# Graph attention on one core: sums of exponentials folded onto half of the partitions by an accumulating transfer, and values half a step later

## The chip, the cores and the metric

The kernel runs on one core of one Trainium2 chip. The core has a matrix engine (TensorE, PE in the profile; PEld is its loading of weights), three engines for elementwise work (VectorE or DVE, ScalarE or ACT, GpSimd or POOL), a queue engine for transfers (SyncE, SP) and sixteen DMA engines that move data. The engines run side by side, each through its own list of instructions in order, and wait for each other by semaphores. SBUF is the working memory, PSUM the memory that TensorE writes; both have 128 partitions. The metric is the time of one execution on the device in microseconds (us). The median of three runs of the kernel before is 3563.94 us (3558.51 to 3566.34).

## The reference, cut to what matters

Two layers over 8 graphs (batches) of N = 2048 nodes with 256 features, all float32. Layer 0 is an attention with 4 heads of 64 features. Its softmax is taken apart over 8 chunks of 256 keys, and the 8 results are added:

```
h = relu(layernorm(x))
q, k, v = h @ Wq.T, h @ Wk.T, h @ Wv.T                 # per head: [N, 64]
scores = clip(q @ kc.T / 8, -10, 10)                   # per chunk j of 256 keys: [N, 256]
scores = where(mask == 0, -10, scores)
attn = softmax(scores, axis=-1)                        # over the 256 keys of one chunk
ctx = sum over j of attn_j @ vc_j                      # [N, 64] per head
x = x + layernorm(ctx @ Wo.T + h) * gamma + beta
```

Layer 1 is a graph attention with one head: weights made of a source and a target term per node, masked by the adjacency, times `h @ W`; its result is added to x.

## The kernel before, in words

**Steps.** For each batch the attention is done in 32 steps: 4 blocks of 512 queries (`nb`) times 8 chunks of 256 keys (`j`). The logits of a step stand transposed: keys on the partitions, queries along the row. A chunk has two key tiles of 128 (`kt`). For one head (`o`, in the order `ORDER`) and one key tile, `logits` (L481) issues four matmuls, each of which reads 64 partitions of k and q (the 64 features of the head) and writes 32 partitions of PSUM. The two heads of a pair lie on partitions 0 to 63 and 64 to 127, so the matmuls of one head occupy one half of TensorE's rows. A float32 matmul is two records in the profile.

**After the logits.** `clip` (L525, VectorE) takes the 128x1024 logits of a head out of PSUM, clips them and applies the mask in one instruction. `exponentials` (L535, ScalarE) works in place. `add` (L541, GpSimd) adds the two key tiles of two heads at a time, 128x1024, into a tile `both` for `sums` (L513): matmuls of 64 partitions each with a matrix of ones give the sum of the exponentials of each head. `values` (L495) multiplies the exponentials by v, again 64 partitions (`half`) at a time and 32 partitions of PSUM per head; the 64 features of a head are two such pieces (`c`), accumulated in two PSUM banks over both halves and both key tiles. `invert` (L547, ScalarE) makes 1/sum by a logarithm and an exponential, `scale` (L553, VectorE) multiplies the values by it, and `gather` (L562) adds the product to the context of the block by a transfer from GpSimd's queue that adds in passing (512 KB). PSUM holds two tiles of logits (`ps_s`), two banks of values (`ps_n`) and two others (`ps_t`).

**The order.** It is written by hand: each engine runs its instructions in the order in which the program issues them. `begin(f)` and `end(f)` (L597, L629) are the two halves of a step: logits of step f-1, half of the values and the sums of step f-2, the other half of the values of step f-3. As two row halves of TensorE must not write one PSUM bank at once, the values of half 0 and half 1 go to different banks and are exchanged in the second turn; `fence` (L460) puts a wait in between. The work between the layers (`Between`, L673) for the block before, and in the first batch half of the search of the adjacency (L312) and the next batch's norms, are pieces with a half-step number `n` in `todo` (L839 and L1127); a piece runs at the end of `begin` or `end`, or ahead of it (`first`, `pe`, `pe1`). For one block these are, by half-step from its end: 5 and 6 `bias`, 8 and 10 `beta`, 18 and 20 `add` on GpSimd; `stats` (two instructions per tile of 128x256), `take` and `flip1` on VectorE; `scaled` and `norm1` on ScalarE; `output_tiled` on TensorE. A block has 16 half-steps, so the blocks 1 to 3 of a batch have pieces and block 0 none but those of the first batch.

**Between the attentions.** After step 31 come the rest of layer 0, then layer 1 (`Layer1.products`, L956) whose matmuls read a tile `g` of [128, 16 x 257]. During its last products `early` (L570) issues the first logits, clips and exponentials of the next batch.

Of the kernel before, what the change touches and what calls it, by code (L numbers as in the profile page):

```python
# [24 lines left out]
SHIFT = 30.0  # L25


@with_exitstack
def gnn_two_layers(
# [97 lines left out]
    class Turning:  # L127
# [3 lines left out]
        def __init__(self, dst, tag):  # L131
            self.dst = dst
            self.squares = work.tile([P, FC * QUADS, TB, Q], F32, tag=tag, name="squares", bufs=3 if tag == "hT" else 2)
# [50 lines left out]
    g = const.tile([P, NT, F + 1], F32, name="g")  # L184
    nc.gpsimd.memset(g[:, :, F:F + 1], 1.0)
# [14 lines left out]
    def load_x(b, nb, tag, bufs):  # L200
        pool = work if tag == "both" else xpool
        t = pool.tile([P, TB, F], F32, tag=tag, name=tag, bufs=bufs)
        nc.sync.dma_start(t, x[b, nb * NB:(nb + 1) * NB, :].rearrange("(p t) f -> p t f", p=P))
        return t

# [61 lines left out]
    def missing_of(rows, t, half):  # L267

        tag = "e" if in_setup[0] else "hn"
        z = work.tile([P, 2 if in_setup[0] else 1, HALF], BF16, tag=tag, name="z", bufs=5)  # L270
# [24 lines left out]
    def keep_bounds(pt, t, half):  # L295

        nb, rows, cols = t // TB, slice(half * 8, (half + 1) * 8), slice((t % TB) * P, (t % TB + 1) * P)
        if nb in bounds:
            dst = bounds[nb][:, rows, cols]
        else:  # L300
            tag = part_tags[(2 * t + half) % 4] if in_setup[0] else "r"
            dst = work.tile([P, 8, P], I8, tag=tag, name="bound_part", bufs=2 if tag == "r" else 1)
# [11 lines left out]
    def adjacency(parts):  # L314
# [15 lines left out]
        turns = [12, 12, 18, 18, 26, 26, 32, 32]  # L330
# [15 lines left out]
    def norm_power(mv, rn):  # L346

        nc.scalar.activation(rn[:, 0, :], mv[:, :, 1], AF.Ln, bias=eps)
        nc.scalar.activation(rn[:, 0, :], rn[:, 0, :], AF.Exp, scale=-0.5)
        nc.scalar.activation(rn[:, 1, :], rn[:, 0, :], AF.Copy, scale=-1.0)  # L350
# [28 lines left out]
    class Projection:  # L379
# [6 lines left out]
        def load(self, nb):  # L386
            self.x[nb] = load_x(self.b, nb, *(("both", 2) if in_setup[0] else ("xp", 1)))
# [81 lines left out]
    class Attention:  # L469
        STEPS = [(nb, j) for nb in range(NNB) for j in range(NCH)]  # L470
# [3 lines left out]
        def __init__(self, proj):  # L474
            self.q, self.k, self.v = proj.q, proj.k, proj.v
            self.before, self.rest = {}, ()
            self.s, self.e, self.both, self.num, self.total, self.rz, self.prod, self.ctxT = ({} for _ in range(8))


# [15 lines left out]
        def values(self, n, half, c, kt):  # L495

            nb, j = self.STEPS[n]
            rows = slice(half * DH, (half + 1) * DH)
            started = (n, c) in self.num
            if not started:  # L500
                self.num[n, c] = ps_n()
            made = []
            for h in range(HEADS):
                p, i = divmod(h, 2)
# [3 lines left out]
                    self.e[n, p][rows, i * KT + kt, :],  # L508
                    start=not started, stop=half == (1 if c else 0) and kt == KT - 1,
                ))  # L510
            return made

        def sums(self, n, half):  # L513
            rows = slice(half * DH, (half + 1) * DH)
            if half:
                self.total[n] = ps_t()
            return [
                nc.tensor.matmul(  # L518
                    self.total[n][h * Q:(h + 1) * Q, :], ones[rows, :], self.both[n, h // 2][rows, h % 2, :],
                    start=half == 1, stop=half == 0,  # L520
                )
                for h in range(HEADS)
            ]

        def clip(self, n, o):  # L525
            nb, j = self.STEPS[n]
            p, i = self.ORDER[o]
            if (n, p) not in self.e:
                self.e[n, p] = work.tile([P, 2 * KT, NB], F32, tag="e", name="e", bufs=5)
            nc.vector.scalar_tensor_tensor(  # L530
                self.e[n, p][:, i * KT:(i + 1) * KT, :], self.s.pop((n, o)), -CLIP * SC,
# [3 lines left out]
        def exponentials(self, n, o):  # L535

            p, i = self.ORDER[o]
            e = self.e[n, p][:, i * KT:(i + 1) * KT, :]
            nc.scalar.activation(e, e, AF.Exp, scale=1.0 / SC)  # L539

        def add(self, n, p):  # L541

            self.both[n, p] = work.tile([P, 2, NB], F32, tag="both", name="both")
            e = self.e[n, p].rearrange("p (i k) q -> p k i q", k=KT)
            nc.gpsimd.tensor_tensor(self.both[n, p], e[:, 0], e[:, 1], op=ALU.add)  # L545

        def invert(self, n):  # L547

            rz = self.rz[n] = work.tile([P, NB], F32, tag="rz", name="rz", bufs=1)
            nc.scalar.activation(rz, self.total.pop(n), AF.Ln)  # L550
            nc.scalar.activation(rz, rz, AF.Exp, scale=-1.0)  # L551

        def scale(self, n, c):  # L553
            nb, j = self.STEPS[n]
            if j == 0 and c == 0:
                self.ctxT[nb] = work.tile([P, 2, NB], F32, tag="ctx", name="ctxT")
            if j > 0 and c == 0:
                self.prod[n] = work.tile([P, 2, NB], F32, tag="prod", name="prod", bufs=1)
            dst = self.ctxT[nb] if j == 0 else self.prod[n]
            nc.vector.tensor_tensor(dst[:, c, :], self.num.pop((n, c)), self.rz[n], op=ALU.mult)  # L560

        def gather(self, n):  # L562
            nb, j = self.STEPS[n]
            if j > 0:
                nc.gpsimd.dma_start(self.ctxT[nb], self.prod.pop(n), accum_op=ALU.add)  # L565
# [4 lines left out]
        def early(self, part):  # L570
# [12 lines left out]
            elif part == 2:  # L583
                self.clip(0, 2)
                self.exponentials(0, 2)
                self.clip(0, 3)
                self.add(0, 0)
            if part == 3:
                for kt in range(KT):
                    self.logits(1, 0, kt)  # L590

        def begin(self, f, pieces=()):  # L597

            self.run(pieces, "first")
            if self.has(f - 3):  # L600
                made = {}
                for kt in range(KT):
                    for half, c in ((0, 0), (1, 1)):
                        made.setdefault(c, []).extend(self.values(f - 3, half, c, kt))
                for c in range(2):
                    fence(self.before.pop((f - 3, c)), made[c])
            if self.has(f - 1):
                self.clip(f - 1, 0)
            if self.has(f - 3):
                self.invert(f - 3)  # L610
            if self.has(f - 2):
                self.exponentials(f - 2, 3)
            if self.has(f - 1):
                self.exponentials(f - 1, 0)
            self.run(pieces, "pe")
            if self.has(f - 1):
                for kt in range(KT):
                    self.logits(f - 1, 1, kt)
                    self.logits(f - 1, 2, kt)
            if self.has(f - 3):  # L620
                self.scale(f - 3, 0)
                self.scale(f - 3, 1)
            if self.has(f - 2):
                self.add(f - 2, 1)
            if self.has(f - 3):
                self.gather(f - 3)
            self.rest = pieces

        def end(self, f, pieces=()):  # L629
            self.run(pieces, "first")  # L630
            if self.has(f - 1):
                self.clip(f - 1, 1)
            self.run(pieces, "pe1")
            if self.has(f - 1):
                self.clip(f - 1, 2)
            self.run(pieces, "after")
            self.run(self.rest, None)
            if self.has(f - 1):
                self.exponentials(f - 1, 1)
                self.exponentials(f - 1, 2)  # L640
            if self.has(f - 2):
                made = {}
                for kt in range(KT):
                    for half, c in ((0, 1), (1, 0)):
                        made.setdefault(c, []).extend(self.values(f - 2, half, c, kt))
                for c in range(2):
                    self.before[f - 2, c] = made[c]
            if self.has(f - 1):
                self.logits(f - 1, 3, 0)
            if self.has(f - 2):  # L650
                sums = self.sums(f - 2, 1)
            if self.has(f - 1):
                self.logits(f - 1, 3, 1)
            if self.has(f):
                self.logits(f, 0, 0)
            self.run(pieces, None)
            self.run(pieces, "pe")
            if self.has(f - 2):
                fence(sums, self.sums(f - 2, 0))
            if self.has(f):  # L660
                self.logits(f, 0, 1)
            if self.has(f - 1):
                self.clip(f - 1, 3)
                self.add(f - 1, 0)
# [8 lines left out]
    class Between:  # L673
# [66 lines left out]
        def power(self):  # L740
            norm_power(self.mv, self.rn)

        def shift(self):
            norm_shift(self.adder, self.mv, self.rn)

        def scaled(self, tiles):
            for t in tiles:
                o = self.o4[:, t, :]
                nc.scalar.activation(
                    o, o, AF.Identity, bias=self.rn[:, 1, t:t + 1], scale=self.rn[:, 0, t:t + 1]  # L750
                )

        def gamma(self, t2):
            o = self.o4[:, 2 * t2:2 * t2 + 2, :]
            self.adder.tensor_tensor(o, o, gamma_r[:, None, :].to_broadcast([P, 2, F]), op=ALU.mult)
# [35 lines left out]
        def flip1(self, t2, tag="hT"):  # L791
            if t2 == 0:
                self.aside = tag == "both"
# [605 lines left out]
```

## Time and profile before

| What | us |
|---|---|
| median of three runs | 3563.94 |
| the profiled execution | 3563.89 |
| its span, first to last instruction | 3562.1 |
| TensorE busy | 3527.6 |
| VectorE busy | 2639.0 |
| ScalarE busy | 1947.4 |
| GpSimd busy | 1808.9 |
| one step of the attention, without pieces on TensorE | 7.72 |
| a step with half of `output_tiled` | 9.45 |
| layer 1's products, per batch | 117.4 |

How to read it. A group line gives the line of the kernel, the engine, the operation, the names written and read, the shape and the count; then the busy time of the group, the mean ns of one, and the engine's idle time just before them with what ended it. A timeline line gives the start, the length, the engine, the line, the operation and how many of them follow each other; in brackets stands the idle time before it and who ended that. A line with two times and a colon is one stretch: its length, the busy time of PE, PEld, DVE, ACT and POOL, the granted TensorE clock (1.00 is full), the share of the DMA engines that was busy, and GB/s. Matmuls are pipelined; many of their records overlap.

### The profile page before, as it was taken

The page shows a single profiled execution, that of the slowest core. Times are in us where ns is not written, and L with a number is a line of the kernel's source. Part 1 is how long each engine was busy: PE and PEld are TensorE (multiplying, and loading weights), DVE is VectorE, ACT ScalarE, POOL GpSimd, SP SyncE. Part 2 cuts the span into 40 slices and gives each one's busy share as a digit, 9 for nine tenths or more (in the row PEclk, how much of TensorE's full clock was granted, in tenths as well). Part 3 has the DMA queues.
Part 4 walks back from the last instruction along what each step waited for, and adds up shares of the span by engine and source line. Part 5 has one row for each costly group of instructions (what it writes and reads, how often), then busy time and mean ns, then how long its engine had stood idle before and what let it go on. Part 6 is the DMA issues. An engine that isn't in the chain of part 4 may idle for free.

```text
span 3562.1 us, 104433 instructions
## 1 busy us (share of the span) xinstructions
PE 3527.6 (99%) x46080; PEld 2183.0 (61%) x46080; DVE 2639.0 (74%) x3979; ACT 1947.4 (55%) x2961; POOL 1808.9 (51%) x1182
## 2 busy tenths in 40 slices
PE   8999999999999999999999999999999999999999
PEld 5455785557755577555775557655586555855568
DVE  7888677867678676786767867678586785757866
ACT  6677426763267633676236762367624766147750
POOL 2688016870278702786037850378404784048731
PEclk9999999999999999999999999999999999999999
DMA  7545423444234441344423444234442434124321
GB/s 234 119 107 134 87 74 85 91 113 91 80 79 85 123 95 60 85 96 109 92 66 85 97 110 91 71 79 91 120 103 55 91 81 118 57 55 91 85 69 48
DMA packets 169111, 329.74 MB, mean 93 GB/s; under 512 B 35664, under 2 KB 97360, under 8 KB 160464
## 3 DMA queue, kind: packets, MB, share of 16 engines
q1 hardware_dynamic: 127696, 203.51, 19.2%
q0 software_dynamic: 32640, 118.50, 18.0%
q8 instruction: 360, 5.90, 0.7%
q10 hardware_dynamic: 8320, 1.05, 0.2%
q14 instruction: 95, 0.78, 0.1%
HBM read 154.14 MB, written 51.43 MB: 58 GB/s over the span
## 4 chain that ended last, share of the span: by engine, by line
PE 97%; DVE 1%; DMA 1%; ACT 1%; issue 0%; POOL 0%; ACTq 0%; DVEq 0%; POOLq 0%; SPq 0%
PE ps_s L490 25%; PE ps_n L506 24%; PE ps_s L963 12%; PE ps_t L518 7%; PE ps_n L963 6%; PE ps_t L963 6%; PE ps_t L714 2%; PE ps_t L434 2%; PE ps_n L434 2%; PE ps_s L434 2%; PE ps_t L814 2%; PE ps_n L814 2%; PE ps_t L448 1%; PE ps_n L448 1%; DVE z L277 0%
## 5 line engine op out<-in xcount | busy, mean ns | idle before, releaser
L530 DVE SCALAR_TENSOR_TENSOR e<-ps_s,bound 128x1024 f32<-128x1024 f32 x1024 | 1224.1, 1220 | 404.0 <-PE ps_s L490 400.6
L545 POOL TENSOR_TENSOR both<-e 128x1024 f32<-128x1024 f32 x512 | 1219.8, 2407 | 571.1 <-PE ps_t L518 355.6
L490 PE MATMUL ps_s<-q,k 64*32 64x512 f32 x16384 | 1431.8, 590 | 1.5 <-DVE e L530 1.4
L539 ACT ACTIVATE e<-e 128x1024 f32<-128x1024 f32 x1024 | 1050.6, 1050 | 481.1 <-DVE e L530 462.7
L506 PE MATMUL ps_n<-e,v 64*32 64x512 f32 x16384 | 1224.9, 591 | 2.4 <-DVE prod L560 2.4
L506 PEld LDWEIGHTS ps_n<-e,v 64*32 64x32 f32 x16384 | 460.9, 107 | 473.1 <-issue 384.1
L490 PEld LDWEIGHTS ps_s<-q,k 64*32 64x32 f32 x16384 | 459.5, 106 | 448.6 <-issue 331.2
L518 PE MATMUL ps_t<-both,ones 64*32 64x512 f32 x4096 | 537.9, 592 | 0.1
L963 PE MATMUL ps_s<-g,w 128*128 128x257 f32 x2048 | 447.8, 380 | 0.0
L963 PEld LDWEIGHTS ps_s<-g,w 128*128 128x128 f32 x2048 | 388.8, 190 | 56.3
L560 DVE TENSOR_TENSOR prod<-ps_n,rz 128x512 f32<-128x512 f32 x448 | 288.5, 686 | 162.8 <-PE ps_n L506 96.1
L986 POOL TENSOR_TENSOR x<-x,r 128x256 f32<-128x256 f32 x124 | 90.7, 745 | 466.2 <-ACT r L984 465.4
L946 DVE SCALAR_TENSOR_TENSOR w<-bound,w 128x1024 f32<-128x1024 int8 x256 | 314.7, 1229 | 8.7
L354 POOL TENSOR_TENSOR krn<-krn,mv 128x4 f32<-128x4 f32 x28 | 6.8, 242 | 575.4 <-DVE w L940 575.4
L963 PE MATMUL ps_n<-g,w 128*128 128x257 f32 x1024 | 292.4, 382 | 0.0
L963 PE MATMUL ps_t<-g,w 128*128 128x257 f32 x1024 | 289.7, 380 | 0.0
L550 ACT ACTIVATE rz<-ps_t 128x512 f32<-128x512 f32 x256 | 152.6, 596 | 229.4 <-PE ps_t L518 201.5
L940 DVE TENSOR_SCALAR w<-src,cd 128x512 f32<-128x512 f32 x512 | 263.1, 556 | 7.0 <-ACT src L921 6.6
L963 PEld LDWEIGHTS ps_n<-g,w 128*128 128x128 f32 x1024 | 192.8, 190 | 44.3 <-issue 17.6
L565 POOL DMA_DIRECT2D ctxT<-prod x224 | 191.0, 853 | 54.1 <-DVE prod L560 46.7
L963 PEld LDWEIGHTS ps_t<-g,w 128*128 128x128 f32 x1024 | 193.8, 189 | 28.2
L551 ACT ACTIVATE rz<-rz 128x512 f32<-128x512 f32 x256 | 161.4, 630 | 8.2
(133 smaller groups left out, 2910.4 us busy)
## 6 DMA issues: line engine op xcount, KB each, us to landing
ctxT<-prod POOLq DMA_DIRECT2D x224, 512.0 KB, 4.9
bound<-bound_d SPq DMA_DIRECT2D x62, 1024.0 KB, 6.2
turned_d<-squares SPq DMA_DIRECT2D x232, 128.0 KB, 2.4
hT<-turned_d SPq DMA_DIRECT2D x58, 512.0 KB, 4.3
rows<-in_adj_dram SPq DMA_DIRECT2D x32, 512.0 KB, 5.3
x<-in_x_dram SPq DMA_DIRECT2D x32, 512.0 KB, 4.9
out_dram<-x SPq DMA_DIRECT2D x31, 512.0 KB, 2.6
xp<-in_x_dram SPq DMA_DIRECT2D x28, 512.0 KB, 4.5
```

The source lines that it names most:

```text
L434: nc.tensor.matmul(in_key_order(pp) if i == 0 else pp, w[:, di, do * P:(do + 1) * P], h, start=di == 0, stop=di == FC - 1,)
L490: nc.tensor.matmul(self.s[n, o][c * Q:(c + 1) * Q, kt, :], self.k[p][rows, at:at + Q], self.q[p][rows, nb * NB:(nb + 1) * NB], start=True, ...
L506: made.append(nc.tensor.matmul(self.num[n, c][h * Q:(h + 1) * Q, :], self.v[rows, j * KT + kt, at:at + Q], self.e[n, p][rows, i * KT + kt, :],
L518: nc.tensor.matmul(self.total[n][h * Q:(h + 1) * Q, :], ones[rows, :], self.both[n, h // 2][rows, h % 2, :], start=half == 1, stop=half == 0,)
L530: nc.vector.scalar_tensor_tensor(self.e[n, p][:, i * KT:(i + 1) * KT, :], self.s.pop((n, o)), -CLIP * SC, bounds[nb][:, j * KT:(j + 1) * K ...
L539: nc.scalar.activation(e, e, AF.Exp, scale=1.0 / SC)
L545: nc.gpsimd.tensor_tensor(self.both[n, p], e[:, 0], e[:, 1], op=ALU.add)
L560: nc.vector.tensor_tensor(dst[:, c, :], self.num.pop((n, c)), self.rz[n], op=ALU.mult)
L565: nc.gpsimd.dma_start(self.ctxT[nb], self.prod.pop(n), accum_op=ALU.add)
L940: nc.vector.tensor_scalar(w[:, i, :], self.src[nb], self.cd[:, 0, j:j + 1], self.cd[:, 1, j:j + 1], op0=ALU.mult, op1=ALU.max,)
L946: nc.vector.scalar_tensor_tensor(two, bounds1[nb][:, j - 1:j + 1, :], 0.0, two, op0=ALU.is_gt, op1=ALU.mult)
L963: nc.tensor.matmul(accs[t][:, 0:F + 1], w[:, i, t * P:(t + 1) * P], g[:, j, :], start=j == 0, stop=j == NT - 1,)
```

## The change

**Sums.** `add` becomes one instruction per head (128x512), written to one of two sides (`both(n)`, the side is n % 2) of a tile [128, 2, 4, 512]. When the four heads of a step are there, `fold` adds the 64 upper partitions to the 64 lower ones or the lower to the upper, by turns from step to step (`side`), with a transfer of [64, 2048] from GpSimd's queue. `sums` then has four matmuls of 64 partitions in place of eight.

**Order.** Logits, values and sums are listed as slots (`o` logits, `v` values, `s` sums; then the index and the key tile). All values of step f-2 now run in step f. Odd steps have 18 slots, even ones 16. The logits and clips run a half-step further ahead: `begin(f)` clips head 3 of step f-1 and head 0 of step f.

**Room.** `g` and the two sides share one buffer by turns (and the first loads of x as well); the exponentials lie in eleven tiles of [128, 2, 512], one per head, in place of five for two heads; `prod` has two buffers.

**Pieces.** The layer norm's mean is subtracted together with the multiplication by gamma, on VectorE (one instruction per tile of 128x256), before ScalarE scales; `shift` and the GpSimd form of `gamma` go. `stats`, `take`, `gamma`, `scaled`, `stats1` and the transposes of the adjacency get other half-steps. A half-step n is now `begin` of f = (n-2)/2 or `end` of f = (n-3)/2.

```diff
-        def values(self, n, half, c, kt):
+        def values(self, n, half, turn, kt):
...
+            c = half ^ turn ^ (n + 1) % 2
...
+        def side(self, n):
+            return 1 - n % 2
+
+        def both(self, n):
+            if self.sides is None:
+                self.sides = g_tile()[:, 0:2 * HEADS * NB].rearrange("p (t h q) -> p t h q", t=2, h=HEADS)
+            return self.sides[:, n % 2]
+
+        def sums(self, n):
+            rows = slice(self.side(n) * DH, (self.side(n) + 1) * DH)
+            self.total[n] = ps_t()
+            for h in range(HEADS):
                 nc.tensor.matmul(
-                    self.total[n][h * Q:(h + 1) * Q, :], ones[rows, :], self.both[n, h // 2][rows, h % 2, :],
-                    start=half == 1, stop=half == 0,
+                    self.total[n][h * Q:(h + 1) * Q, :], ones[rows, :], self.both(n)[rows, h, :],
+                    start=True, stop=True,
                 )
...
+                nc.gpsimd.tensor_tensor(self.both(n)[:, 2 * p + i, :], e[:, 0, :], e[:, 1, :], op=ALU.add)
+
+        def fold(self, n):
+            if self.has(n):
+                mine, other = (slice(i * DH, (i + 1) * DH) for i in (self.side(n), 1 - self.side(n)))
+                nc.gpsimd.dma_start(self.both(n)[mine], self.both(n)[other], accum_op=ALU.add)
...
         def begin(self, f, pieces=()):
...
+            odd = f % 2
             self.run(pieces, "first")
...
             self.run(pieces, "pe")
...
+            if odd:
+                if f > 1:
+                    self.slots(f - 1, "o01")
+                self.slots(f, "v00", "v01", "v10")
+            else:
+                self.slots(f, "v00", "v10", "v01", "v11")
+            if f > 1:
+                self.clip(f - 1, 3)
+            self.clip(f, 0)
+            self.exponentials(f - 1, 3)
+            self.exponentials(f, 0)
+            if f == 1:
+                for o in range(3):
+                    self.add(0, o)
+            self.add(f - 1, 3)
+            self.fold(f - 1)
+            if odd:
+                self.slots(f, "o10", "v11", "o11", "o20")
+            else:
+                self.slots(f, "o10", "s00", "o11", "o20")
+                self.add(f, 0)
+            self.run(pieces, None)
 
         def end(self, f, pieces=()):
+            odd = f % 2
             self.run(pieces, "first")
...
+            if odd:
+                self.slots(f, "s00", "o21", "v20", "v30", "v21", "v31")
+                self.add(f, 0)
+            else:
+                self.slots(f, "v20", "o21", "v21", "v30")
+            self.clip(f, 1)
+            self.clip(f, 2)
+            self.invert(f - 2)
+            self.exponentials(f, 1)
+            self.exponentials(f, 2)
+            self.add(f, 1)
             self.run(pieces, "pe1")
...
+            if odd:
+                self.scale(f - 2)
+                self.slots(f, "o30", "o00", "o31", "o01")
+            else:
+                self.slots(f, "o30", "v31")
+                self.scale(f - 2)
+                self.slots(f, "o31", "o00")
+            self.gather(f - 2)
+            self.add(f, 2)
             self.run(pieces, None)
             self.run(pieces, "pe")
...
+        def gamma(self, tiles):
+            for t in tiles:
+                o = self.o4[:, t, :]
+                nc.vector.scalar_tensor_tensor(
+                    o, o, self.mv[:, t, 0:1], gamma_r, op0=ALU.subtract, op1=ALU.mult
+                )
...
+                8: [lambda: self.beta(0)],
+                9: [pe1(lambda: self.output_tiled(0))],
...
+                10: [
+                    pe(lambda: self.output_tiled(1)), lambda: self.take(0), lambda: self.take(1),
+                    lambda: self.beta(1),
                 ],
...
+                11: [lambda: self.stats([0, 1])],
+                12: [lambda: self.stats([2, 3])],
+                13: [self.power],
+                14: [lambda: self.gamma([0, 1])],
+                15: [lambda: self.gamma([2, 3])],
+                16: [lambda: self.scaled(range(TB))],
                 18: [lambda: self.add(0)],
                 20: [lambda: self.add(1)],
...
+            at(22, lambda: self.stats1([0, 1]))
+            at(24, lambda: self.stats1([2, 3]))
             at(26, self.power1)
             at(27, self.shift1)
             at(28, lambda: self.norm1(0))
...
-            w = work.tile([P, 4, NB], F32, tag="e", name="w", bufs=5)
...
+                w = work.tile([P, 2, NB], F32, tag="e", name="w", bufs=ES)
```

The flips (`flip1`) keep the half-steps 30 and 31, `bias` 5 and 6.

## The prediction

> **What bounds the kernel now.** The page's busy times come first, then its chain of work that ended last, to learn which engine sets the end.
>
> ```profile
> PE 3527.6 (99%) x46080; PEld 2183.0 (61%) x46080; DVE 2639.0 (74%) x3979; ACT 1947.4 (55%) x2961; POOL 1808.9 (51%) x1182
> PE 97%; DVE 1%; DMA 1%; ACT 1%; issue 0%; POOL 0%; ACTq 0%; DVEq 0%; POOLq 0%; SPq 0%
> ```
>
> TensorE is never idle; the chain is TensorE's own work. A change pays only by taking work from it, and costs wherever it makes it wait. The groups give the prices:
>
> ```profile
> L530 DVE SCALAR_TENSOR_TENSOR e<-ps_s,bound 128x1024 f32<-128x1024 f32 x1024 | 1224.1, 1220 | 404.0 <-PE ps_s L490 400.6
> L545 POOL TENSOR_TENSOR both<-e 128x1024 f32<-128x1024 f32 x512 | 1219.8, 2407 | 571.1 <-PE ps_t L518 355.6
> L518 PE MATMUL ps_t<-both,ones 64*32 64x512 f32 x4096 | 537.9, 592 | 0.1
> L565 POOL DMA_DIRECT2D ctxT<-prod x224 | 191.0, 853 | 54.1 <-DVE prod L560 46.7
> ```
>
> One step in TensorE's timeline shows how its two row halves share the work:
>
> ```profile
> 704.80 0.61 PE L490 MATMUL ps_s<-q,k 64*32 64x512 f32 x4
> 704.90 0.61 PE L506 MATMUL ps_n<-e,v 64*32 64x512 f32 x4
> ...
> 705.23 0.61 PE L490 MATMUL ps_s<-q,k 64*32 64x512 f32 x4
> ...
> 705.33 0.61 PE L518 MATMUL ps_t<-both,ones 64*32 64x512 f32 x4
> ```
>
> Four records start together (one per 32-column group) and the same half takes the next four 0.43 us later, the other half running 0.10 beside it. Call a set of four matmuls (eight records) a slot: 0.86 us of one half, so 0.43 us of a filled array. A step has 8 slots of logits, 8 of values and 2 of sums: 18 x 0.43 = 7.74. VectorE's timeline gives what its 1220 ns really take in a row:
>
> ```profile
> 2354.14 2.35 DVE L530 SCALAR_TENSOR_TENSOR e<-ps_s,bound 128x1024 f32<-128x1024 f32 x2 [0.36 <-PE ps_s L490]
> 2357.57 1.22 DVE L530 SCALAR_TENSOR_TENSOR e<-ps_s,bound 128x1024 f32<-128x1024 f32 x1 [1.08 <-PE ps_s L490]
> 2359.03 1.23 DVE L530 SCALAR_TENSOR_TENSOR e<-ps_s,bound 128x1024 f32<-128x1024 f32 x1 [0.24 <-PE ps_s L490]
> 2360.20 1.29 DVE L560 TENSOR_TENSOR prod<-ps_n,rz 128x512 f32<-128x512 f32 x2
> 2363.59 2.35 DVE L530 SCALAR_TENSOR_TENSOR e<-ps_s,bound 128x1024 f32<-128x1024 f32 x2 [2.10 <-PE ps_s L490]
> 2365.86 1.28 DVE L728 TENSOR_TENSOR o<-ps_t,hn 128x512 f32<-128x512 f32 x2
> ```
>
> The second clips of steps lie 7.72 apart. VectorE waits 1.08 + 0.24 + 0.36 us a step: room into which the pieces between the layers (stats, take, flips) fall for nothing. Two clips occupy 2.27 us (2363.59 to 2365.86); two scales 1.21. Last, whole blocks of eight steps, one without such pieces (seven intervals) and one with all of them:
>
> ```profile
> 2284.40:2338.70 54.30, 54.30 (x1012) 26.94 (x1004) 42.04 (x43) 36.69 (x42) 35.69 (x19) 1.00 0.37 89
> 2404.20:2469.40 65.20, 65.20 (x1292) 34.95 (x1276) 54.87 (x68) 48.51 (x66) 54.22 (x34) 1.00 0.41 91
> ```
>
> In the second, VectorE is busy 54.87 and GpSimd 54.22 of 65.20: reserves of only 16% or so. The granted clock is 1.00, so nothing is to be had there. The profiled execution's own time is 3563.89 us (span 3562.1), the median 3563.94; sums are made against 3564.
>
> **The gain.** Sums go from two slots to one (2048 records fewer). The halves take it by turns, so an odd step has 9 slots on each half and an even one 8: 17 slots, 7.31 us. 256 steps x 0.43 = **-110 us**. That is all TensorE can win.
>
> At each even-to-odd turn the order puts two slots of one half behind each other. In the lines above, logits at 704.80 start before values at 704.90 that stand ahead of them in the program: each half runs its own queue, so I charge nothing (bound: the 0.10 offset x 128 = 13). The Trainium skill, "TensorE: Matmul & The Clock Gate" (The mechanism), instead has matmuls start strictly in program order; by it those 13 us would be paid. The row decides.
>
> **VectorE (-110 needs it on time).** In an even step, from the end of the second logits to the end of the fourth lie 4 slot pairs, 3.43 us. VectorE has two clips and two scales there, 2.27 + 1.21 = 3.48: no room. From the fourth logits to the second of the next step it has 3.43 against 2.27: room 1.16. TensorE tolerates nothing: three pairs (2.57) separate a logits end from the slot that reuses its PSUM, and the two clips take 2.35 plus 0.13 until they start. So pieces run in a step's first half fit up to 1.16, but a piece at the end of an even step is paid in full. There stand stats of two tiles (half-step 11: 0.42 + 0.18 per tile, pitch 1.15 for two) and the new gamma (15). Gamma moves from GpSimd to VectorE; the nearest row is L971, four in 1.66, so two take 0.83. In the second and third block with pieces a flip (0.65) falls beside each gamma: the first half then has 1.48 against 1.16 (0.3 late), the end 1.48. Per batch (1.15 + 0.83) + 2 x (1.15 + 0.3 + 1.48) = 7.8; x8 = **+62** (bounds 30, if half is absorbed by waits elsewhere, and 90). In the first batch eight searches of the adjacency (L277, 1.78 each) also stand at ends: 1.2 to 1.7 each in place of today's cover, **+12** (0 to 20). Behind a late clip queue the exponentials, adds and the fold.
>
> **GpSimd.** Four adds of 512 replace two of 1024. Rows: 2.38 per 1024; 0.695 per 256 (L986, four in 2.78). The line through both gives 1.26; plain halving 1.19, the mean row L735 1.51. With 1.26 a step is 5.04, plus two issues of 0.86, plus gaps 0.1: 6.9 of 7.31, room 0.4. Removed: gamma (two of 1.3 a block), shift. Kept: bias, beta, add, six of 1.27 a block, four of them in the first three steps of the second and third block: 5.1 against 1.2 of room. The fold is issued behind them, the sums wait for it and TensorE's queue for the sums. The folds' slack (below) takes most; 1.5 us a block remain: 16 x 1.5 = **+24** (0 to 60).
>
> **The fold's landing.** The trace has no transfer like it. For an even step's tile: after its fourth logits a clip (0.13 + 1.14), the exponential (0.1 + 1.0), the add (0.1 + 1.26); the fold is issued 3.8 us on. Its sums stand 11 pairs = 9.44 on in TensorE's order, so a landing of up to 5.4 us from issue (0.2 left for queue and wake) is hidden; an odd step's has a pair more. Nearest row: the gather, also 512 KB by GpSimd's queue with addition: 4.9 us median, by the transfer records its last packet 4.2 (quickest twentieth) to 5.7 (slowest) after issue, and once 6.9 in the chain. Ends: 4.2, and 8.0 if 64 partitions engage half of the transfer engines (4.9 and once more the 3.1 that the gather's packets take). I take the gather's spread, as bytes and queue are the same, now with twice the traffic: a fifth of 128 folds over by 0.5, and the crowded blocks a little worse, **+20** (0 to +330, which is 2.6 x 128). Against the change speaks the Trainium skill, "SBUF — State Buffer" (Door 1): partitions 0 to 63 reach only 8 of 16 ports, 196 GB/s at 1 MiB where 128 partitions have 328. By it 512 KB would take an estimated 2.7 us of packets, no more than the gather's 3.1; the row would stand.
>
> **Other parts.** ScalarE: four normalising activations (2.06 us in a row) now precede an invert once a block, delaying scales by 0.2: **+5**. Start of a batch: step 1 has eight logits slots and no values, paced by clips; before, values ran in the same step. One clip more is exposed at most (1.2), against work of the layer before: **+6** in all (-10 to +25). End of a batch: the last fold lands beside the next batch's q and k (two times 3.6 us of matmuls), nothing; without them in the last batch at most 3. Buffers (`g` shared by turns, eleven small `e`) add waits that end before TensorE's. Two `prod` buffers remove the scales' wait for the gather (50.1 us in all, under TensorE): nothing.
>
> **Sum:** -110 + 62 + 12 + 24 + 20 + 5 + 6 = +19: 3564 + 19 = **3583 us**.
>
> **Rivals.**
> *Hidden pieces (faster).* If VectorE's pieces at the ends cost nothing, because TensorE comes late to them by its own waits: 3583 - 62 = 3521. For it: today all of them are covered. Against: the 3.48 against 3.43. It decides once 26 of the 62 are hidden.
> *GpSimd becomes the bound.* Adds at 1.51 make 6.04 + 1.72 = 7.8 a step. A block without pieces then takes 62, as now; the later blocks 62 + 7.6 = 69.7 against 65.5: about 3640. For it: the 128x512 rows' means; against: these overlap the instruction before.
> *The fold lands late.* At 8.0 us: 3454 + 333 + some 45 left of the other terms = 3830; at 6.0 it is 3583 + 77.
>
> **How the numbers follow.** My sum's case 0.42, its own range 3545 to 3640; hidden pieces 0.33; GpSimd 0.10; late fold 0.10; else 0.05. The range 3495 to 3720 leaves out a nearly full gain and a fold of over 7 us. About 0.2%, 7 us, is what measurement tells from no change. Faster: 0.31 of the hidden pieces, 0.06 of my case, 0.01: 0.38. Same: 0.08. Slower: 0.54.
>
> **What would show it.** Right: sums x2048; plain blocks at 7.3 to 7.45 a step; steps long by 1 to 1.5 us where stats or gamma close an even step; ps_s weight loads waiting for VectorE. GpSimd near 95% in attention. Wrong: waits of ps_t on the fold in most even steps (landing above 5.4), or adds above 1.4, or a piece block near 62.

## The result, and the profile after

The changed kernel takes 3782.29 us in the median (3774.23 to 3785.24, four runs) against 3564.41 before: a ratio of 1.061, 95% interval [1.0589, 1.0632]. The sign of the forecast was right, by a thin margin (+19 of 3564, with a chance of 0.54 for slower); the time, 3583 in a range of 3495 to 3720, was not. The profiled execution of the changed kernel took 3785.24 us, its span is 3783.5.

The busy times and the chain of the changed kernel's page:

```profile
PE 3549.0 (94%) x44032; PEld 2085.4 (55%) x44032; DVE 2715.3 (72%) x4083; ACT 1948.6 (52%) x2929; POOL 2066.2 (55%) x1885
PE 11%; DMA 2%; DVE 1%; POOL 1%; issue 0%; ACT 0%; POOLq 0%; DVEq 0%; ACTq 0%
```

The 2048 records are gone (46080 to 44032), yet TensorE is busy 21 us longer and idle for 234 us where it was idle for 34. The chain covers 15% of the span, so it names no culprit; the groups and the waits do. Columns of a group: busy us, mean ns of one | idle us before, and what ended most of it.

```profile
L564 POOL TENSOR_TENSOR g<-e 128x512 f32<-128x512 f32 x1024 | 1466.5, 1483 | 473.2 <-ACT e L557 218.1
L502 PE MATMUL ps_s<-q,k 64*32 64x512 f32 x16384 | 1511.2, 602 | 90.6 <-DVE e L549 89.9
L549 DVE SCALAR_TENSOR_TENSOR e<-ps_s,bound 128x1024 f32<-128x1024 f32 x1024 | 1215.0, 1218 | 517.0 <-PE ps_s L502 497.4
...
L539 PE MATMUL ps_t<-g,ones 64*32 64x512 f32 x2048 | 284.1, 622 | 95.7 <-DMA g<-g 91.3
```

Two waits that did not exist: the sums wait 91.3 us for the fold (`g<-g`), the logits 89.9 us for clips. By stage, over the eight batches: the block without pieces is 24 us longer than before, the three blocks with pieces 48, 48 and 52, the end of a batch (from step 31's third clip to its last values) 46.

A third loss stands in no wait. Columns of the windows: us, busy time of PE, PEld, DVE, ACT, POOL with counts, granted clock, DMA share, GB/s.

```profile
2600.00:2650.00 50.00, 43.85 (x748) 19.46 (x736) 38.41 (x43) 34.66 (x49) 39.56 (x36) 0.93 0.74 149
2650.00:2700.00 50.00, 46.03 (x817) 21.50 (x802) 40.14 (x53) 33.11 (x48) 39.66 (x36) 0.97 0.73 139
```

The granted clock is no longer 1.00. The trace has 31 spells of half clock in the changed kernel, 4 before, each 3.41 us or a multiple; they cost 63 us against 9. They lie on a fixed grid of 3.41 us: a window of it in which TensorE was busy for less than about 1.5 us is followed by one at half clock. All the emptier ones are, with one at 1.51 the first that is not; of 17 windows with 1.5 to 1.75 us five are, of the 1064 fuller ones eight. So a gap of about 2 us costs its length, and 1.7 us more if it lies within one window.

### Where the two waits come from

A gap ahead of logits, at step 31 of the last batch. VectorE and GpSimd in the timeline (start, us):

```profile
3603.64 2.34 DVE L549 SCALAR_TENSOR_TENSOR e<-ps_s,bound 128x1024 f32<-128x1024 f32 x2
3605.90 1.27 DVE L588 TENSOR_TENSOR prod<-ps_n,rz 128x512 f32<-128x512 f32 x2
3607.10 0.69 DVE L138 STREAM_TRANSPOSE squares<-hn 128x512 f32<-128x512 f32 x1
3607.72 2.61 DVE L767 SCALAR_TENSOR_TENSOR o<-o,mv,gamma_r 128x256 f32<-128x256 f32 x2
3610.26 2.34 DVE L549 SCALAR_TENSOR_TENSOR e<-ps_s,bound 128x1024 f32<-128x1024 f32 x2
```

```profile
3607.48 0.87 POOL L592 DMA_DIRECT2D ctxT<-prod  x1
3608.08 1.56 POOL L564 TENSOR_TENSOR g<-e 128x512 f32<-128x512 f32 x1
```

Two gammas (L767) take 2.61 us, not 0.83; the first alone 2.21, and it ends 0.3 us after GpSimd's add does. The two clips behind them are late, and TensorE stands for 2.71 us, until 3611.52:

```profile
3611.52 1.08 PE L502 MATMUL ps_s<-q,k 64*32 64x512 f32 x4 [2.71 <-DVE e L549]
```

The tile's own view gives all of them (ns, minimum/median/maximum):

```profile
L767 DVE SCALAR_TENSOR_TENSOR o<-o,mv,gamma_r x128: 439/480/2403, 216.3 to 3665.2; 128x256 f32<-128x256 f32 x128
```

44 of them take over 0.7 us, together 58 us more than 0.41 each. All 44 end 0.28 to 0.30 us after one of GpSimd's adds (L564). 24 of them began while such an add ran; the 20 longest, 2.21 us and more, began 0.07 to 0.25 us into the issue of a gather (L592), with an add behind it, as in the lines above. Gamma reads two operands from SBUF; the clip, which reads one there and one in PSUM, keeps its 1218 ns.

A gap ahead of sums, at step 9 of the seventh batch. SyncE's fetch of the next block's bounds, GpSimd's fold, and TensorE:

```profile
2946.56 0.32 SPq L176 DMA_DIRECT2D bound<-bound_d  x1
```

```profile
2948.33 0.83 POOL L569 DMA_DIRECT2D g<-g  x1 [0.29 <-POOL g L564]
```

```profile
2957.91 0.63 PE L539 MATMUL ps_t<-g,ones 64*32 64x512 f32 x4 [2.63 <-DMA g<-g]
```

The fetch waits for the buffer that the last clip of a block frees, so it starts some 2 us ahead of that step's fold. The transfers' view (KB, median us from issue to landing):

```profile
g<-g POOLq DMA_DIRECT2D x256, 512.0 KB, 5.6
ctxT<-prod POOLq DMA_DIRECT2D x224, 512.0 KB, 5.2
bound<-bound_d SPq DMA_DIRECT2D x62, 1024.0 KB, 6.9
```

A fold lands in 5.64 us (5.1 in the quickest twentieth); those of steps 7, 15, 23 and 31, beside a fetch or the stores of a batch's end, in 8.1 to 8.8. (Such figures by step are medians over the second to the eighth batch; in the first the fetches stand elsewhere.)

### The profile page after: what moved, and what is told of

It is laid out like the page before. It is cut to its first block, busy times and chain, and to the rows that moved or that the text cites. A ratio compares the mean times of both kernels' runs of the same rounds, so it can differ in the third digit from the quotient of the medians.

```text
span 3783.5 us, 101129 instructions
## 1 busy us (share of the span) xinstructions
PE 3549.0 (94%) x44032; PEld 2085.4 (55%) x44032; DVE 2715.3 (72%) x4083; ACT 1948.6 (52%) x2929; POOL 2066.2 (55%) x1885
## 5 line engine op out<-in xcount | busy, mean ns | idle before, releaser
L564 POOL TENSOR_TENSOR g<-e 128x512 f32<-128x512 f32 x1024 | 1466.5, 1483 | 473.2 <-ACT e L557 218.1
L502 PE MATMUL ps_s<-q,k 64*32 64x512 f32 x16384 | 1511.2, 602 | 90.6 <-DVE e L549 89.9
L549 DVE SCALAR_TENSOR_TENSOR e<-ps_s,bound 128x1024 f32<-128x1024 f32 x1024 | 1215.0, 1218 | 517.0 <-PE ps_s L502 497.4
L557 ACT ACTIVATE e<-e 128x1024 f32<-128x1024 f32 x1024 | 1064.7, 1053 | 666.4 <-DVE e L549 638.9
L517 PE MATMUL ps_n<-e,v 64*32 64x512 f32 x16384 | 1374.9, 601 | 12.3 <-ACT r L1009 7.6
L502 PEld LDWEIGHTS ps_s<-q,k 64*32 64x32 f32 x16384 | 469.1, 107 | 669.0 <-issue 300.0
L517 PEld LDWEIGHTS ps_n<-e,v 64*32 64x32 f32 x16384 | 472.7, 108 | 433.6 <-issue 246.8
L539 PE MATMUL ps_t<-g,ones 64*32 64x512 f32 x2048 | 284.1, 622 | 95.7 <-DMA g<-g 91.3
L569 POOL DMA_DIRECT2D g<-g x256 | 212.8, 831 | 78.9 <-POOL g L564 63.8
L592 POOL DMA_DIRECT2D ctxT<-prod x224 | 206.0, 920 | 76.7 <-DVE prod L588 57.1
```

The costliest lines, as they stand in the source:

```text
L502: nc.tensor.matmul(self.s[n, o][c * Q:(c + 1) * Q, kt, :], self.k[p][rows, at:at + Q], self.q[p][rows, nb * NB:(nb + 1) * NB], start=True, ...
L517: made.append(nc.tensor.matmul(self.num[n, c][h * Q:(h + 1) * Q, :], self.v[rows, j * KT + kt, at:at + Q], self.e[n, self.ORDER.index((h / ...
L539: nc.tensor.matmul(self.total[n][h * Q:(h + 1) * Q, :], ones[rows, :], self.both(n)[rows, h, :], start=True, stop=True,)
L549: nc.vector.scalar_tensor_tensor(self.e[n, o], self.s.pop((n, o)), -CLIP * SC, bounds[nb][:, j * KT:(j + 1) * KT, :], op0=ALU.max, op1=ALU ...
L557: nc.scalar.activation(self.e[n, o], self.e[n, o], AF.Exp, scale=1.0 / SC)
L564: nc.gpsimd.tensor_tensor(self.both(n)[:, 2 * p + i, :], e[:, 0, :], e[:, 1, :], op=ALU.add)
```

## The experiments

All times are medians of four runs with the ratio to the kernel before on the same chip. TensorE's waits behind them, from the profiled execution of each (us between its first and last matmul in which none ran, by the instruction that came next; "clock" is the time lost to half clock):

| run | time | ratio, 95% | sums | logits | all idle | clock |
|---|---|---|---|---|---|---|
| before | 3564 | 1 | 0 | 2 | 25 | 9 |
| after | 3782 | 1.061 | 96 | 91 | 225 | 63 |
| no_fold | 3644 | 1.022 [1.0205, 1.0236] | 0 | 120 | 149 | 38 |
| unread | 3677 | 1.032 [1.0306, 1.0340] | 0 | 112 | 161 | 40 |
| fold_small | 3697 | 1.037 [1.0355, 1.0390] | 30 | 117 | 178 | 47 |
| gamma_out | 3719 | 1.042 [1.0408, 1.0441] | 107 | 36 | 178 | 48 |
| one_input | 3717 | 1.043 [1.0407, 1.0461] | 106 | 46 | 186 | 50 |
| gamma_pool | 3710 | 1.041 [1.0393, 1.0431] | 104 | 35 | 172 | 40 |
| floor | 3519 | 0.988 [0.9865, 0.9895] | 0 | 36 | 64 | 12 |
| unread_gp | 3612 | 1.013 [1.0118, 1.0148] | 1 | 34 | 113 | 36 |

### The fold: its landing or its load

```
-            self.fold(f - 1)
```

> Left out: the transfer that adds one half of the partial sums to the other, so the sums cover half of the keys. In the changed kernel TensorE is idle 234 us, of which its sums wait 91.3 us for the transfer; 27 spells of half clock more than before cost another 54 us. Theory A (the landing of the transfer is the largest loss): the 91 us and about ten of the spells (10 x 1.7) go, and GpSimd is given back 0.85 us a step: 3782 - 91 - 17 = 3674, or less where late clips came from late sums. Theory B (VectorE's pieces are the limit, and a wait for the transfer only stands where a wait for a clip would stand without it): half of it comes back as waits for clips, 3782 - 50 = about 3730.

3644.26: theory A, and more of it, -138. The sums' wait is gone, but the logits wait 29 us more:

```profile
L502 PE MATMUL ps_s<-q,k 64*32 64x512 f32 x16384 | 1477.7, 601 | 119.6 <-DVE e L549 118.0
...
L539 PE MATMUL ps_t<-g,ones 64*32 64x512 f32 x2048 | 269.1, 596 | 0.0
```

To tell the landing from the load, the transfer was kept and turned round, so that it adds into the rows that nobody reads:

```
-                nc.gpsimd.dma_start(self.both(n)[mine], self.both(n)[other], accum_op=ALU.add)
+                nc.gpsimd.dma_start(self.both(n)[other], self.both(n)[mine], accum_op=ALU.add)
```

> The transfer runs as in the changed kernel, at the same place and with the same bytes, but adds into the half that the sums do not read, so the sums cover half of the keys and wait only for the last add. Theory A (the price is the wait for the landing): as without the transfer, 3644, within 15. Theory B (the price is GpSimd's issue of 0.83 us a step and the traffic): most of the 138 stays, above 3720.

3676.89, between the two: waiting for the landing costs 105 us, the load of the transfer (issue, traffic) the other 33. The sums no longer wait:

```profile
L539 PE MATMUL ps_t<-g,ones 64*32 64x512 f32 x2048 | 271.6, 597 | 0.3 <-POOL g L564 0.3
```

Next the transfer moves two of the four heads only:

```
-self.both(n)[mine], self.both(n)[other]
+self.both(n)[mine, 0:2, :], self.both(n)[other, 0:2, :]
```

> Left out: the transfer of two of the four heads; it moves 256 KB a step, not 512, its count and its place stay. Theory A (the landing is packets: some 2.7 of 5.6 us): it lands 1.3 us sooner, so the even steps without pieces no longer wait (0.4 now), and of the 96 us that sums wait 25 to 35 stay, where the issue itself is late: about 3710. Theory B (the landing is fixed cost from issue to first packet): sums wait 80 us or more, about 3770.

3696.62, theory A:

```profile
g<-g POOLq DMA_DIRECT2D x256, 256.0 KB, 4.2
```

Half the bytes land 1.4 us sooner (183 GB/s for the difference), the blocks without pieces lose their waits for sums (18.8 to 0.9 us), and 86 us are won. The sums that start as soon as their fold has landed (within 0.2 us) fall from 124 to 39 of 256, so most paths are short by less than those 1.4 us. The 196 GB/s at 1 MiB for partitions 0 to 63, from which the prediction made its estimate after the Trainium skill, "SBUF — State Buffer" (Door 1), lies 7% above this slope.

### Gamma on VectorE

```
-                14: [lambda: self.gamma([0, 1])],
-                15: [lambda: self.gamma([2, 3])],
```

> Left out: in the blocks beside attention, the subtraction of the mean and the product with gamma that the change put on VectorE (48 pairs of instructions of 128x256). In the changed kernel 24 of the steps that hold them end in a gap of TensorE of 2.3 to 2.7 us, most of them followed by a spell of half clock. Theory A (an instruction that reads two operands from SBUF stands still while GpSimd adds, and the long gap then costs clock as well): the gaps of the second pair shrink by 2.2 or so and some 14 spells behind them go: 24 x 2.2 + 14 x 1.7 = 77, so about 3705. Theory B (VectorE pays the 0.83 us a pair that an undisturbed row gives, and the rest of the gap is the flip or the clips): 48 pairs x 0.83 = 40 at most, half of them in a half step with room: about 3760.

3719.14, near theory A (21 of the 24 steps had such a gap, not all). What holds the instruction up is told by putting another of the same length into its place:

```
+                if self.nb < NNB - 1:
+                    nc.vector.bn_stats(small.tile([P, 6], F32, tag="stats", name="stats"), o)
+                    continue
                 nc.vector.scalar_tensor_tensor(
                     o, o, self.mv[:, t, 0:1], gamma_r, op0=ALU.subtract, op1=ALU.mult
```

> In the three blocks beside attention each of the 96 gamma instructions is replaced by a statistics instruction over the same 128x256 tile (0.40 us in this case's rows, as long as a gamma that isn't held up, 0.44). Left out with it: mean and gamma there. VectorE's queue stays as long; the one difference is that it reads one operand from SBUF, not two. Theory A (two SBUF operands stand still while GpSimd adds): the 44 gammas of 1.1 to 2.4 us, 58 us over what the others take, have no like; only the plain price stays, so 3719 (gamma left out) + 24 x 0.4 = about 3730. Theory B (any instruction at this place is held up, by the queue or by a wait the trace doesn't name): about 3780.

3717.39, theory A; VectorE's queue is as long, and none is held up:

```profile
L768 DVE BATCH_NORM_STATS2 stats<-o 128x6 f32<-128x256 f32 x96 | 34.6, 401 | 0.0
```

This instruction also differs in operation and writes less; but the clip is gamma's operation, writes 128x1024 to SBUF, reads one operand there, and isn't held up either (1184 to 1254 ns). So it is the number of SBUF operands that decides, beside a GpSimd that adds. The Trainium skill, "SBUF — State Buffer" (Who interferes with whom), says it: a VectorE instruction with two SBUF inputs contends with a GpSimd instruction that reads SBUF, and the second one blocks. The 24 that began during an add agree; in the 20 longest gamma's record starts 0.36 to 0.54 us before the add's, during the issue of the gather, and whether the issue holds them is not shown. The plain time of these instructions, 0.83 a pair in the prediction, cost nothing that can be measured (3717 beside 3719).

```
-                13: [self.power],
-                14: [lambda: self.gamma([0, 1])],
-                15: [lambda: self.gamma([2, 3])],
-                16: [lambda: self.scaled(range(TB))],
+                13: [self.power_p],
+                14: [self.shift],
+                15: [lambda: self.scaled_p(range(TB))],
+                16: [lambda: self.gamma_p(0)],
+                17: [lambda: self.gamma_p(1)],
```

> One part of the change undone: in the three blocks beside attention gamma goes back to GpSimd (two products of 128x512 a block, and the small shift), with the order of the kernel before (power, shift, scaling on ScalarE, then gamma). Theory A (VectorE's stand was the costlier place): VectorE's part falls as with gamma left out, -63; GpSimd has 3.1 us more a block and issues two or three folds later, 24 x 1 to 1.5 us of waits for sums: 3745. Theory B (GpSimd is at its limit, so folds slip by the whole 3.1 us and longer gaps cost half clock too): 24 x 3.1 + 20 = 95 against 63, 3815.

3709.89: the whole work, 72 us faster than the changed kernel, better than either theory. Folds are issued up to 7.3 us after the start of the fourth clip in the crowded steps (5.6 in the changed kernel), but the sums' wait grows by 8 us only:

```profile
L502 PE MATMUL ps_s<-q,k 64*32 64x512 f32 x16384 | 1522.1, 594 | 35.3 <-DVE e L549 34.5
...
L539 PE MATMUL ps_t<-g,ones 64*32 64x512 f32 x2048 | 277.5, 608 | 104.1 <-DMA g<-g 94.6
```

### Both, and GpSimd behind them

The edits of no_fold and gamma_pool in one kernel, then those of unread and gamma_pool.

> Left out: the fold (the sums cover half of the keys); and gamma goes back to GpSimd. Theory A (the two losses add): 3644 - 72 = 3572, so the new order without its transfer and without its move of gamma just reaches the kernel before; what is left over the 3454 of a full gain is the batches' ends, the statistics at ends of even steps, the searches of the first batch, and clock. Theory B (they overlap: one waits where the other did): 3600 or more.

3519.03: neither theory. Together they win 263 us, where alone they won 138 and 72. With both gone the new order is 1.2% faster than the kernel before, but it leaves half of the keys out of the sums.

```profile
L502 PE MATMUL ps_s<-q,k 64*32 64x512 f32 x16384 | 1473.2, 593 | 36.2 <-DVE e L549 34.7
```

> As unread, and gamma on GpSimd as in the kernel before. Theory A (only the wait costs): 3519, as with the transfer left out, within 15; GpSimd has its 0.83 us a step and 3.1 us a block more and still nobody waits for it. Theory B (GpSimd becomes the bound once the sums do not wait): it is then busy 5.04 + 1.7 of 6.9 to 7.3 us a step and its pieces stand out: 24 blocks x 3 us, 3590.

3611.63, near theory B: nobody waits for the fold, and still it costs 93 us beside floor. Values now wait for scales, and a gather for the one before it:

```profile
L517 PE MATMUL ps_n<-e,v 64*32 64x512 f32 x16384 | 1392.9, 596 | 38.4 <-DVE prod L588 28.4
```

```profile
2579.43 0.88 POOL L592 DMA_DIRECT2D ctxT<-prod  x1 [2.20 <-DMA ctxT<-prod]
```

In steps 16 to 19 the fold is issued 9.4 to 11.8 us after the start of its clip: GpSimd is the bound there. That fits the sum of 263: without the fold GpSimd has 1.1 us a step more (0.83 of issue and 0.29 of waiting for its own add), room for gamma.

### GpSimd's pieces

Bias, beta and the residual's addition are left out in the three blocks:

```
-                5: [lambda: self.bias(0)],
-                6: [lambda: self.bias(1)],
-                8: [lambda: self.beta(0)],
...
-                    lambda: self.beta(1),
...
-                18: [lambda: self.add(0)],
-                20: [lambda: self.add(1)],
```

> Left out: the six additions of 128x512 that GpSimd does for the layers' end in each of the three blocks beside attention (output bias, beta, residual). Theory A (GpSimd's backlog delays the folds, as the prediction had it with 24 us): the waits for sums of the three blocks, 55 us, fall to the level of a block without pieces, 3 x 18 less 10 for the batch start, about 30; with some spells of half clock -35: about 3745. Theory B (the folds are late by their landing and by other transfers, and GpSimd catches up between its pieces): -10 at most.

3769.66, ratio 1.0569 [1.0547, 1.0591]: -13, theory B or close to it, and at the edge of noise (the intervals overlap by 0.0002). In the changed kernel the backlog is small beside the landing.

### The ends of a batch

```
-            at(STEPS2 + 2, pe(lambda: ahead.tiles()), pe(lambda: ahead.qk(0, 0, ps_h)))
+            at(STEPS2 + 2, ahead.tiles, lambda: ahead.qk(0, 0, ps_h))
```

> In the last steps of a batch the first q and k products of the next batch are issued behind the values of the step, not ahead of them, so ScalarE's evictions of them no longer stand ahead of the last exponentials. Theory A (the exponential of the last step waits behind these evictions, 3.9 us in place of 1.4; add, fold and sums follow, and TensorE waits 1 to 6 us for the last sums): the 21 us idle there go, with five or six spells of half clock: 3782 - 21 - 10 = 3751. Theory B (the end of a batch is bound by its chain of products and transfers anyway): no change.

3771.80, ratio 1.0559 [1.0527, 1.0591]: -10, a third of theory A and again at the edge of noise. The last fold is issued 4.0 us after the start of its clip in place of 6.6, but lands in 10.2 us beside the stores and fetches there; of 21 us of waiting 11 are left.

```
+            if unfinished:
+                unfinished()
+                unfinished = None
             att.begin(f, todo.pop(2 * f + 2, []))
-            if unfinished:
-                unfinished()
-                unfinished = None
```

> The end of the layer before (reciprocals, relus, additions) is issued ahead of step 1's begin, so GpSimd's four additions for it stand ahead of the adds and the fold of step 0. Theory A (at the start of a batch ScalarE's relus wait up to 9.7 us for GpSimd, and the exponentials behind them hold TensorE's values, 1.43 us in six batches): -9 to -15, 3770. Theory B (the adds of step 0 wait for the end of the products in any case, and the relus would now stand ahead of the exponentials): within 5 us of the changed kernel's time.

3799.02, ratio 1.0652 [1.0628, 1.0675]: slower by 17, worse than either theory. The values' wait is gone, but the first block's waits for sums rise from 19 to 37 us: the fold of step 0 is later still, and the waits behind it rise from 8 to 27 us.

### The fetches beside the fold, and whole kernels

```
-        at(PER + 4, lambda: fetch(bounds, 2))
...
+            (PER + 6, bounds, 2, 0), (PER + 10, bounds, 2, 1), (2 * PER + 6, bounds, 3, 0), (2 * PER + 10, bounds, 3, 1),
...
+        nc.scalar.dma_start(of[nb][:, rows, :], bound_d[nb][:, rows, :])
...
-                -3: [self.load],
+                -2: [first(lambda: self.load())],
```

> The megabyte of bounds that each block fetches starts, in the changed kernel, as soon as the last clip of the block before has freed its buffer, 2 us ahead of the fold of steps 7, 15, 23 and 31; these folds land 8.1 to 8.8 us after issue (median over the batches) where the others take 5.6. Here it is issued in two halves by ScalarE, in its order, three and five steps later, and the loads of x by ScalarE a half step later. Theory A (the folds of these steps are late because of the fetch): they land at 5.6, and the gaps ahead of the sums two steps later, 1 to 3.4 us in each of four places a batch, 62 us in all, shrink to 0.4: -45, with some ten spells of half clock -17: about 3720. Theory B (GpSimd's backlog or the bytes in all set the landing, so other folds slip instead): 3770 or more.

3794.23, ratio 1.0647 [1.063, 1.0664], theory B: the folds of steps 7, 15 and 23 do land in 5.3 to 5.7 now, as theory A has it, but half a fetch is now issued some 0.4 us after the late folds of steps 16 and 24, which land in 8.4, and gaps of 2.5 to 5.8 us stand before their sums. That a fetch beside a fold makes it late is shown at both places; that moving it helps is not.

The edits of gamma_pool and tail_order together:

> All of the reference's work: gamma on GpSimd and the q and k products of a batch's end behind the values. Theory A (what is left is the landing: sums wait 0.3 us in even steps and 1 to 3 us where a transfer of the bounds runs beside the fold, with half clock behind the long ones): 3710 - 10 - 5 = 3695. Theory B (the end of a batch and the blocks trade waits): 3710.

3703.98, ratio 1.0394 [1.0379, 1.0410], the best median with all of the work, between the theories; the interval overlaps that of gamma_pool. The same with the moved fetches:

> All of the reference's work, with three edits together: gamma back on GpSimd, the q and k products at a batch's end behind the values, and the fetches of bounds and x by ScalarE at later steps. Theory A (the parts add): 3782 - 72 - 10 - 60 = 3640. Theory B (with gamma back, GpSimd issues folds late in three steps a block, and the fold's waits come back there): 3680.

3733.81, ratio 1.0477 [1.0443, 1.0510], slower than either theory: the fetches' move costs 30 here. No whole kernel beat the one before.

## Why the prediction was right or wrong

**The gain (-110): right in floor, lost for the most part in the changed kernel.** In floor the second and third block of a batch, idle time and clock taken off, are 24 and 22 us shorter than before, where 64 steps x 0.43 = 27.5 were expected. In the changed kernel the whole span without idle time and clock falls by 33 us only (3528.5 to 3495.6; floor 3439.3). So the 221 us by which its span grew are 200 of idle time and 54 of clock, less these 33, and 77 of the expected gain stand in no gap. Part of that is time in which one half of TensorE runs alone (below).

**The fold's landing (+20): the step that failed most.** The path was nearly right: from the start of the fourth clip to the issue the prediction's terms make 3.6 us, the trace 4.0, of which 0.29 are the fold's wait for its own add. But the landing was taken from the gather's 4.9, as the same bytes by the same queue; it is 5.64, over the limit of 5.4 that the text had set itself. A fifth of 128 folds was to come late; 124 of the 256 sums start as soon as their fold has landed. The trace before had a sign of it: the longest of its gathers, 8.68 us, has a fetch of bounds issued 0.9 us behind it. And what else is under way came in as "twice the traffic" alone: a block's bounds are fetched beside its last fold, and of the 96 us in which all of TensorE waits for sums 60 belong to steps 7, 15, 23 and 31. The measured price is 105 us. The late-fold rival was the right one; at 6.0 us it gave +77.

**VectorE at the ends of even steps (+62): the place was right, the prices were not.** Statistics, 1.15 each in the sum, leave gaps of 0.62 where nothing else holds TensorE, 14 us in 23 gaps. Gamma, at 0.83 a pair from the row of an instruction that ran beside no GpSimd add, costs 72 us when undone. Of the hidden-pieces rival this much holds: one_input's instructions, as long as an undisturbed gamma, cost nothing that can be measured; the statistics were not hidden.

**GpSimd (+24): within its range, 13** without the six additions a block, and its adds follow each other every 1.27 us as predicted (the 1483 ns are overlapping records). Its room of 0.4 a step did not count the fold's 0.29 of waiting for its own add; unread_gp shows how soon it is the next bound.

**The first batch's searches (+12): right**, seven gaps of 0.7 to 2.2 us behind them, 10 in all, and some half clock. ScalarE's +5 no run separates.

**Start and end of a batch (+6 and nothing): wrong.** At the start three gaps of 1.29, 1.44 and 1.15 us recur, some 24 us over seven batches. Two waits were missed:

```profile
POOL g L564 <- PE ps_t L988: 217.8, 7, 31.4
...
ACT r L1009 <- POOL x L1011: 76.0, 30, 9.7
```

The adds of step 0 wait until all products are done, since these read the `g` whose place the sides take, and ScalarE's relus wait for the additions behind those adds. At the end ScalarE's exponential stands behind the evictions of q and k, so the last fold is late: 21 us.

**The clock: missing.** "The granted clock is 1.00, so nothing is to be had there" was true of the kernel before. 54 us of the loss are half clock behind gaps. The Trainium skill, "TensorE: Matmul & The Clock Gate" (Why this matters for your kernels), warns of gaps over about 3 us; here gaps of 2 to 2.7 were enough where they fell into one window.

**The half-order flips (nothing): right, as far as floor shows.** In 107 of its 112 turns from an even to an odd step (step 5 on) the values start ahead of the logits that the kernel issues before them, by 0.27 us in the median: the two halves do not start strictly in the order of issue, as the prediction's row had it. Counted by the starts of the records (each is given 0.43 us of its half, 0.85 at half clock; stretches with other matmuls are left aside), one half runs alone for 50 us of the steps in the kernel before and for 66 in floor, which has the same flips. In the changed kernel it is 139, in gamma_pool 139, in unread 92, in no_fold 82: what is more goes with the wait for the fold. If a half alone is worth half of TensorE, these 89 us more make 44 of the missing 77; the rest stays open.

## What to carry to other kernels

On a saturated engine a wait costs more than its length where it costs clock too, and taking two losses away can win more than both apart (263 us here against 138 and 72). Take the price of a moved instruction from a row that runs beside the same neighbours as it will (gamma: 0.41 alone, up to 2.4 beside GpSimd's adds), and a transfer's landing from what else is under way then. A path that is shorter than its transfer's landing was not made good here by moving other work about it.

## What was not expected of the hardware

- Half clock follows a 3.41-us window in which TensorE was busy for less than about 1.5 us, and lasts one such window; no gap of 3 us is needed.
- An accumulating transfer of 512 KB from 64 partitions to 64 lands in 5.6 us, one of 128 partitions to 128 in 5.2; 256 KB of the first kind in 4.2. A fetch of 1 MB beside it adds about 2.6.
- A VectorE instruction of 128x256 with two SBUF operands takes 0.44 us or, beside GpSimd's 1.27-us adds, up to 2.40, and ends 0.3 us after the add.
